# The last image of a window-attention block with a dynamic convolution: its mean and taps computed ahead, two convolution pieces as diagonal products

## The chip, the cores and the metric

The kernel runs on one core of a Trainium2 chip. The time is the device time of one execution in microseconds, the median over several runs. A core has five engines, each with a queue of its own: TensorE (PE, with its weight loads as PEld), VectorE (DVE), ScalarE (ACT), GpSimd (POOL) and SyncE (SP), which here only issues DMAs. ScalarE can issue DMAs too.

## The reference

```python
# layer 0: on x (16, 192, 56, 56), a shifted-window block (7x7 windows, 6 heads)
x1 = shortcut + window_attention(layernorm(x))
y  = gelu(layernorm(x1) @ fc1_w + fc1_b)           # 768 hidden channels
x  = x1 + (y @ fc2_w + fc2_b)
# layer 1: a depthwise 3x3 convolution whose taps depend on the image
pooled = x.mean(axis=(2, 3))                       # per image and channel
t  = relu(batchnorm(pooled @ w1.T))                # 48 values
wt = t @ w2.T + b2                                 # 9 taps per channel,
wt = wt * MASK                                     # of which 4 survive
out = depthwise_conv(x, wt, padding=1) + bias
```

The mask keeps the three taps of the row above and the left neighbour. So every output element is a bias and four products, and no output of an image can be computed before the mean over its whole final x is known. All data are fp32.

## The kernel before

The 16 images are cut into 4 units each (`NU`), 64 units in all. The 192 channels are 3 groups (`G`) of 64; the 128 partitions hold 64 channels of two halves of the image, 28 rows each (`LR`). So `x`, the residual and later the convolution's input, is a tile of 128 x 3 groups x 29 rows x 56, where row 0 is the halo: the last row of the other half, copied by two DMAs (L885). A unit is 7 rows of both halves.

The main loop (L1364 on) is a software pipeline over units: in round r it computes scores of unit r, the weighted sum and projection of r-1, the first MLP layer of r-2 (L783, GELU on ScalarE L795 into `hid`) and the second MLP layer of r-3 (L821, for each group 6 steps of two products, then on VectorE the update of x, L808, which also leaves the sum over the unit in `sums`). When the last unit of an image is through, `taps` follows: VectorE adds the unit sums to `pooled` (L843), TensorE multiplies by `w1` (L850), VectorE makes the taps `wt` (L861 to L879), and SP copies the halos (L885). Then `conv` runs for six pieces (half hf of the rows, group g), 14 rows of each partition: ScalarE writes the first tap with the bias (L911), VectorE adds the other three (L935, `scalar_tensor_tensor`, both inputs and the output in SBUF), ScalarE sets one row that lies at the top edge back to the bias (L928, pieces with hf = 1), and SP stores the piece in two or three DMAs (L948). For the last image there is nothing left to overlap with; its pieces are written into `hid`, which is free after the second layer has read it.

No engine's order is written down directly. Each step is an entry of `Plan` with an engine, a duration (its author's estimate), and the keys it reads and writes; `Plan.order` simulates the engines with these durations. TensorE keeps the order in which entries were added; on every other engine the step that could start first goes first, then the one that is due first. So durations and keys of an entry decide the order of all engines, and each engine then runs its list strictly in that order.

Of the kernel before, what the change touches and what calls it, by code (L numbers as in the profile page):

```python
# [45 lines left out]
class Plan:  # L46
# [95 lines left out]
def tile_swin_then_dynamic_conv(  # L142
# [37 lines left out]
    def sb(name, *shape):  # L180
        return const.tile(list(shape), F32, tag=name, name=name)
# [40 lines left out]
    m2 = sb("m2", 128, HT)  # L222
    rs = sb("rs", 128, HT)
    sums = [sb(f"sums{i}", 128, G, NU) for i in range(2)]
    pooled = sb("pooled", 128, G)
    trow = sb("trow", 128, RED)
    prod = sq.rearrange("p g t -> p (g t)")[:, 0 : G * NTAP * RED]
# [29 lines left out]
    def P(j):  # L257
        return slice(64 * j, 64 * j + 64)

    def X(s):  # L260

        b, u = divmod(s, NU)
        return [("x", b % 3, u, i) for i in range(3)]
# [534 lines left out]

            add("ACT", 0.95, go, [pk, "b1f", "table"], [("hid", f)])

    def second_layer(s):
        b, u = divmod(s, NU)
        xv = rows(s).rearrange("p g r c -> p g (r c)")
        for g in range(G):
            p, pk = bank()

            def ends(p=p, g=g):
                nc.vector.scalar_tensor_tensor(  # L808
                    xv[:, g],
                    p[:, 0, 0:UT],  # L810
                    vecs[:, 5, g : g + 1],
                    xv[:, g],
                    ALU.add,
                    ALU.add,
                    accum_out=sums[b % 2][:, g, u : u + 1],
                )

            for f in range(NFC):
                def product(p=p, g=g, f=f):
                    for ab in range(2):  # L820
                        nc.tensor.matmul(  # L821
                            p[P(ab), 0, 0:UT],
                            wf2[:, f, g * 64 : (g + 1) * 64],
                            hid[:, f, ab],
                            start=(f == 0),
                            stop=(f == NFC - 1),
                            tile_position=(0, 64 * ab),
                        )

                add("PE", 0.66, product, [("hid", f), ("wf2", f // 2)], [pk])  # L830
                if f == NFC - 1:
                    add("DVE", 0.65, ends, [pk, "vecs"], X(s) + [("sums", b % 2)])


    def taps(b):


        p, pk = bank()
        sl = b % 3
        add(  # L840
            "DVE",
            0.2,
            lambda: nc.vector.tensor_reduce(pooled, sums[b % 2], AX.X, ALU.add),  # L843
            [("sums", b % 2)],
            ["pooled"],
        )

        def product():
# [24 lines left out]
        w = wt[b % 2].rearrange("p g t -> p (g t)")  # L873

        def fin():
            nc.vector.tensor_reduce(
                w.rearrange("p (k o) -> p k o", o=1), prod, AX.X, ALU.add
            )
            nc.vector.tensor_tensor(w, w, b2t.rearrange("p g t -> p (g t)"), ALU.add)  # L879

        add("DVE", 0.9, fin, ["sq", "b2t"], [("wt", b % 2)])
        t = xt[sl]
        for to, of, row in ((0, 1, LR), (1, 0, LR)):
            def go(to=to, of=of, row=row):
                nc.sync.dma_start(t[P(to), :, 0, :], t[P(of), :, row, :])  # L885
            add("SP", 0.65, go, X(b * NU + NU - 1), [("halo", sl, to)], lag=2.5)

    pieces = [(hf, g) for hf in range(2) for g in range(G)]

    def conv(b, i):  # L890
        hf, g = pieces[i]
        sl = b % 3
        yi = (b * 6 + i) % 2
        y, yk = yt[yi], ("y", yi)
        if b == B - 1:

            y = hid[:, i].rearrange("p a (r c) -> p (a r) c", c=IMG)
            yk = ("hid", i)
        nr = LR // 2
        src = xt[sl][:, g]  # L900
        prev = src[:, nr * hf : nr * hf + nr]
        same = src[:, nr * hf + 1 : nr * hf + nr + 1]
        w = wt[b % 2]
        keys = [k for u in range(NU) for k in X(b * NU + u) if u // 2 == hf or u == 2 * hf - 1]
        if hf == 0:
            keys += [("halo", sl, 0), ("halo", sl, 1)]
        keys.append(("wt", b % 2))
        add(
            "ACT",
            1.05,  # L910
            lambda: nc.scalar.activation(  # L911
                y, prev, AF.Identity, bias=vecs[:, 6, g : g + 1], scale=w[:, g, 1:2]
            ),
            keys + ["vecs"],
            [yk],
        )
        for t, dst, s_ in (
            (0, y[:, :, 1:], prev[:, :, : IMG - 1]),
            (2, y[:, :, : IMG - 1], prev[:, :, 1:]),
            (3, y[:, :, 1:], same[:, :, : IMG - 1]),  # L920
        ):
            if t == 3 and hf == 1:

                r = IMG - SHIFT - LR - nr
                add(
                    "ACT",
                    0.35,
                    lambda: nc.scalar.activation(  # L928
                        y[64:128, r], zero[64:128], AF.Identity, bias=vecs[64:128, 6, g : g + 1]
                    ),  # L930
                    ["vecs", "zero"],
                    [yk],
                )
            def go(t=t, dst=dst, s_=s_):
                nc.vector.scalar_tensor_tensor(  # L935
                    dst, s_, w[:, g, t : t + 1], dst, ALU.mult, ALU.add
                )
            add("DVE", 1.4, go, keys, [yk])
        ch = slice(g * 64, g * 64 + 64)
        parts = [(0, 0, nr, SHIFT + nr * hf)]  # L940
        first = SHIFT + LR + nr * hf
        n = min(nr, IMG - first)
        parts.append((1, 0, n, first))
        if n < nr:
            parts.append((1, n, nr, 0))
        for h, lo, hi, at in parts:
            def go(h=h, lo=lo, hi=hi, at=at):
                nc.sync.dma_start(out[b, ch, at : at + hi - lo, :], y[P(h), lo:hi])  # L948
            add("SP", 0.65, go, [yk], [], lag=12.0)

    def table(name):
        add("ACT", 1.3, lambda: nc.scalar.preload_act_table_set(name), [], ["table"])
# [408 lines left out]
    def has(s):  # L1361
        return 0 <= s < S

    for r in range(-2, S + 3):  # L1364
# [57 lines left out]
        if norms:  # L1422
            deviations(norms)
        b, k = divmod(r - 3, NU)
        if k == NU - 1 and 0 <= b < B:
            taps(b)
        for b in range(B):
# [87 lines left out]
```

## Time and profile before

| | us |
|---|---|
| median of 3 runs | 2835.39 (2834.74 to 2842.21) |
| the profiled execution | 2838.8 |
| its span, first to last instruction | 2837.0 |
| PE busy | 2771.9 (98%) |
| DVE busy | 1857.8 (65%) |
| POOL busy | 1605.6 (57%) |
| ACT busy | 1562.2 (55%) |
| mean granted TensorE clock | 0.99 |

The span counts from the first to the last instruction that the profiler saw. The page says for each group of instructions how long one takes on the mean, how long its engine stood idle in front of it, and what ended that idle time; its chain of work that ended last says which engine the end hung on. The stretches view gives busy times between two moments of the span, with the clock that was granted to TensorE there (1.0 is full speed) and the DMA share. Waiting of an engine that nothing hangs on costs nothing.

### The profile page before, as it was taken

The page shows a single profiled execution, that of the slowest core. Times are in us where ns is not written, and L with a number is a line of the kernel's source. Part 1 is how long each engine was busy: PE and PEld are TensorE (multiplying, and loading weights), DVE is VectorE, ACT ScalarE, POOL GpSimd, SP SyncE. Part 2 cuts the span into 40 slices and gives each one's busy share as a digit, 9 for nine tenths or more (in the row PEclk, how much of TensorE's full clock was granted, in tenths as well). Part 3 has the DMA queues.
Part 4 walks back from the last instruction along what each step waited for, and adds up shares of the span by engine and source line. Part 5 has one row for each costly group of instructions (what it writes and reads, how often), then busy time and mean ns, then how long its engine had stood idle before and what let it go on. Part 6 is the DMA issues. An engine that isn't in the chain of part 4 may idle for free.

```text
span 2837.0 us, 79158 instructions
## 1 busy us (share of the span) xinstructions
PE 2771.9 (98%) x34241; PEld 1718.4 (61%) x34241; DVE 1857.8 (65%) x3129; ACT 1562.2 (55%) x2338; POOL 1605.6 (57%) x1424
## 2 busy tenths in 40 slices
PE   7899999999999999999999999999999999999995
PEld 5566666666566666566566566566566566566552
DVE  5565675767677586675767666576675767667564
ACT  3545556556556456556556556456555556556452
POOL 5564565565565565565665565565665665665530
PEclk9899999999999999999999999999999999999997
DMA  6312232323313324233333313324133332313121
GB/s 128 81 28 48 54 76 60 78 63 73 84 37 79 74 56 90 47 73 70 73 67 73 82 37 81 72 58 90 41 74 74 73 69 67 81 40 76 43 52 50
DMA packets 122229, 189.32 MB, mean 67 GB/s; under 512 B 31208, under 2 KB 96664, under 8 KB 121880
## 3 DMA queue, kind: packets, MB, share of 16 engines
q1 hardware_dynamic: 117512, 184.24, 29.2%
q8 instruction: 269, 4.41, 0.7%
q10 hardware_dynamic: 4368, 0.02, 0.1%
q14 instruction: 80, 0.66, 0.1%
HBM read 66.81 MB, written 38.98 MB: 37 GB/s over the span
## 4 chain that ended last, share of the span: by engine, by line
PE 96%; DVE 1%; DMA 1%; issue 1%; POOL 0%; ACT 0%; SPq 0%; ACTq 0%; DVEq 0%; POOLq 0%
PE ps L783 27%; PE ps L821 27%; PE ps L469 14%; PE ps L654 9%; PE ps L746 5%; PE ps L690 5%; PE ps L549 4%; PE ps L732 3%; PE ps L318 2%; DVE hid L935 0%; PE ps L850 0%; POOL xs L425 0%; SPq L1236 0%; ACT q L506 0%; PE ps L1115 0%
## 5 line engine op out<-in xcount | busy, mean ns | idle before, releaser
L821 PE MATMUL ps<-hid,wf 128*64 128x392 f32 x4608 | 772.5, 494 | 0.8 <-ACT o L717 0.8
L783 PE MATMUL ps<-xs,wf 64*128 64x392 f32 x4608 | 771.2, 490 | 2.1 <-POOL xs L454 2.1
L783 PEld LDWEIGHTS ps<-xs,wf 64*128 64x128 f32 x4608 | 446.5, 187 | 315.9 <-POOL xs L454 3.6
L821 PEld LDWEIGHTS ps<-hid,wf 128*64 128x64 f32 x4608 | 327.2, 137 | 411.2 <-issue 386.2
L302 POOL TENSOR_TENSOR fold<-sq 128x392 f32<-128x392 f32 x128 | 131.5, 1027 | 577.9 <-PE ps L318 509.7
L795 ACT ACTIVATE hid<-ps,b1f 128x784 f32<-128x784 f32 x384 | 341.5, 913 | 170.7 <-PE ps L783 168.6
L590 POOL TENSOR_TENSOR e<-e,top 128x784 f32<-128x784 f32 x192 | 306.2, 1610 | 216.4 <-DVE top L585 216.4
L469 PE MATMUL ps<-xs,wqkv 64*128 64x392 f32 x2304 | 404.0, 502 | 10.6 <-POOL xs L436 9.7
L935 DVE SCALAR_TENSOR_TENSOR y<-x,wt,y 128x770 f32<-128x770 f32 x270 | 329.5, 1234 | 86.1 <-ACT y L911 49.6
L482 ACT ACTIVATE q<-ps,qbs 128x400 f32<-128x400 f32 (+1 forms) x128 | 68.4, 589 | 493.6 <-PE ps L469 493.6
L608 POOL TENSOR_TENSOR e<-e,tot 128x784 f32<-128x784 f32 x192 | 307.3, 1614 | 49.3 <-DVE tot L603 47.1
L469 PEld LDWEIGHTS ps<-xs,wqkv 64*128 64x128 f32 x2304 | 221.6, 190 | 173.5 <-issue 18.6
L654 PE MATMUL ps<-wqkv,xs 64*64 64x192 f32 x6144 | 276.4, 325 | 0.0
L302 POOL TENSOR_TENSOR fold<-x 128x392 f32<-128x392 f32 x128 | 131.5, 1027 | 254.1 <-PE ps L318 166.7
L454 POOL TENSOR_TENSOR xs<-x,rb 128x392 f32<-128x392 f32 x192 | 236.9, 1261 | 30.1 <-DMA rb<-rsd 30.1
L717 ACT COPY o<-ps 32x392 f32<-32x392 f32 x512 | 246.5, 481 | 9.0 <-PE ps L690 2.7
L619 DVE STREAM_TRANSPOSE tt<-e 128x512 f32<-128x512 f32 x384 | 246.3, 685 | 5.1 <-POOL e L608 3.6
L654 PEld LDWEIGHTS ps<-wqkv,xs 64*64 64x64 f32 x6144 | 224.6, 133 | 29.0 <-issue 15.4
L575 DVE TENSOR_TENSOR e<-ps,bt 128x784 f32<-128x784 f32 x192 | 175.1, 968 | 99.2 <-PE ps L549 99.0
L770 DVE SCALAR_TENSOR_TENSOR x<-ps,pbt,x 128x196 f32<-128x196 f32 (+2 forms) x576 | 156.1, 344 | 96.5 <-PE ps L732 93.0
L602 DVE TENSOR_REDUCE tot<-e 128x16 f32<-128x784 f32 x192 | 180.4, 939 | 34.4 <-ACT e L597 34.3
L425 POOL TENSOR_TENSOR xs<-x,rb 128x343 f32<-128x343 f32 x192 | 186.5, 999 | 24.4 <-PE ps L654 17.4
(105 smaller groups left out, 3236.9 us busy)
## 6 DMA issues: line engine op xcount, KB each, us to landing
pt<-tt SPq DMA_DIRECT2D x256, 192.0 KB
x<-in_x_dram SPq DMA_DIRECT2D x112, 294.0 KB
out_dram<-y SPq DMA_DIRECT2D x135, 196.0 KB
pt<-tt SPq DMA_DIRECT2D x256, 96.0 KB
rb<-rsd SPq DMA_DIRECT2D x118, 196.0 KB
out_dram<-y SPq DMA_DIRECT2D x45, 154.0 KB
x<-in_x_dram SPq DMA_DIRECT2D x16, 168.0 KB
pt<-tt SPq DMA_DIRECT2D x128, 12.0 KB
```

The costliest lines, as they stand in the source:

```text
L302: nc.gpsimd.tensor_tensor(f, src[:, 0], src[:, 1], ALU.add)
L454: nc.gpsimd.tensor_tensor(xs2[:, g], xv[:, g], rb[:, 1], ALU.mult)
L469: nc.tensor.matmul(p[:, ab, 0:UT], lhs_qk(ab, g, i), d[P(ab), g, 0:UT], start=(g == 0), stop=(g == G - 1), tile_position=(64 * ab, 0),)
L590: nc.gpsimd.tensor_tensor(ev, ev, top[j].broadcast_to([128, 16, N]), ALU.subtract)
L608: nc.gpsimd.tensor_tensor(ev, ev, tot[j].broadcast_to([128, 16, N]), ALU.mult)
L619: nc.vector.transpose(tt[:, kb, 16 * j : 16 * j + 16], src)
L654: nc.tensor.matmul(p[P(w % 2), ab, i * DIM : (i + 1) * DIM], d[P(ab), g, w * N : w * N + 64], wqkv[P(ab), g, 2 * DIM :], start=(g == 0), s ...
L717: add("ACT", 0.5, lambda dst=dst, src=src: nc.scalar.copy(dst, src), [k], [("o", j, i)])
L783: nc.tensor.matmul(p[:, ab, 0:UT], wf1[P(ab), g, f * 128 : (f + 1) * 128], xs2[P(ab), g], start=(g == 0), stop=(g == G - 1), tile_position ...
L795: nc.scalar.activation(hid[:, f], p[:, :, 0:UT], AF.Gelu, bias=b1f[:, f : f + 1])
L821: nc.tensor.matmul(p[P(ab), 0, 0:UT], wf2[:, f, g * 64 : (g + 1) * 64], hid[:, f, ab], start=(f == 0), stop=(f == NFC - 1), tile_position= ...
L935: nc.vector.scalar_tensor_tensor(dst, s_, w[:, g, t : t + 1], dst, ALU.mult, ALU.add)
```

## The change

Only the last image is concerned; the instructions of all others keep their order.

1. *Early mean.* The mean of the last image no longer waits for the second layer's results. With the second layer linear, the sum over the last unit of `x + hid @ wf2 + fc2_b` is the sum of x (`xsum`, reduced before the update), plus the sum of each hidden channel (`hsum`, six reductions) times `wf2`, plus the bias times the number of positions. TensorE does 18 products of one column for it, between groups 0 and 1 of the second layer; the product with `w1` goes between groups 1 and 2.
2. *Dependences by group.* A piece of the convolution waits for its own group of x (`("fin", g)`) instead of for all of it.
3. *Two pieces on TensorE.* Pieces (1,1) and (0,2) are computed as four matmuls per 7 rows, with a diagonal 128 x 128 matrix of the tap as weights, shifted x as the moving side, accumulated in PSUM; ScalarE moves them to `hid` with the bias. GpSimd makes the eight diagonals from an identity and the taps. For (1,1) the row at the top edge is set to the bias by ScalarE and one row of VectorE puts its left-neighbour tap back.
4. *Stores on two queues.* These two pieces are stored by DMAs that ScalarE issues, the other four by SP.
5. *Durations* of the last image's VectorE steps go from 1.4 to 0.95 in the plan, the lag of its stores from 12 to 4, and the pieces are added in the order (1,1), (0,2), (1,0), (1,2), (0,0), (0,1).

As built, VectorE's list at the end reads: group 0's update, the product added to `pooled`, group 1's update, the taps, first step of (1,0), group 2's update, second step of (1,0), first and second of (1,2), third of (1,0), third of (1,2), first and second of (0,0), the row of (1,1), third of (0,0), the three of (0,1). ScalarE's reads: first tap of (1,0), of (1,2), their edge rows, first tap of (0,0), eviction and edge row of (1,1), first tap of (0,1), three stores of (1,1), eviction of (0,2), its two stores.

```diff
+    def early_mean(b):
+        s = b * NU + NU - 1
+        xv = rows(s).rearrange("p g r c -> p g (r c)")
+        for f in range(NFC):
+            add("DVE", 0.85, lambda f=f: nc.vector.tensor_reduce(
+                hsum[:, f : f + 1], hid[:, f].rearrange("p a t -> p (a t)"), AX.X, ALU.add),
+                [("hid", f)], [("hsum", f)])
+        add("DVE", 1.3, lambda: nc.vector.tensor_reduce(xsum, xv, AX.X, ALU.add), X(s), ["xsum"])
+        def go():
+            nc.vector.tensor_reduce(pooled, sums[b % 2][:, :, 0 : NU - 1], AX.X, ALU.add)
+            nc.vector.tensor_tensor(pooled, pooled, xsum, ALU.add)
+            nc.vector.scalar_tensor_tensor(
+                pooled, vecs[:, 5], float(UT), pooled, ALU.mult, ALU.add)
+        add("DVE", 0.5, go, [("sums", b % 2), "xsum", "vecs"], ["pooled"])
+        yield
+        p, pk = bank()
+        def product():
+            for g in range(G):
+                for f in range(NFC):
+                    nc.tensor.matmul(p[0:64, 0, g : g + 1], wf2[:, f, g * 64 : (g + 1) * 64],
+                        hsum[:, f : f + 1], start=(f == 0), stop=(f == NFC - 1),
+                        tile_position=(0, 0))
+        add("PE", 1.3, product, [("hsum", f) for f in range(NFC)], [pk])
+        add("DVE", 0.2, lambda: nc.vector.tensor_tensor(
+            pooled[0:64], pooled[0:64], p[0:64, 0, 0:G], ALU.add), [pk], ["pooled"])
...
+    def conv_product(b, i, unit, uk, room, dk):
+        hf, g = pieces[i]
...
+        for t in range(NTAP):
+            add("POOL", 0.35, lambda t=t: nc.gpsimd.tensor_scalar(
+                diag[:, t], unit, w[:, g, t : t + 1], None, ALU.mult),
+                uk + [("wt", b % 2)], dk if t == 0 else [("diag", g, t)])
+        p, pk = bank()
+        def product():
+            for j in range(2):
+                o = p[:, j, 0:UT].rearrange("p (r c) -> p r c", c=IMG)
+                r0 = nr * hf + j * WS
+                prev, same = src[:, r0 : r0 + WS], src[:, r0 + 1 : r0 + 1 + WS]
+                for k, (t, dst, s_) in enumerate((
+                        (1, o, prev),
+                        (0, o[:, :, 1:], prev[:, :, : IMG - 1]),
+                        (2, o[:, :, : IMG - 1], prev[:, :, 1:]),
+                        (3, o[:, :, 1:], same[:, :, : IMG - 1]))):
+                    nc.tensor.matmul(dst, diag[:, t], s_, start=(k == 0), stop=(k == NTAP - 1),
+                        skip_group_check=True)
...
+        add("PE", 5.3, product, keys, [pk])
+        add("ACT", 0.95, lambda: nc.scalar.activation(
+            y.rearrange("p (a r) c -> p a (r c)", a=2), p[:, :, 0:UT], AF.Identity,
+            bias=vecs[:, 6, g : g + 1]), [pk, "vecs"], [yk])
...
+        stores(b, hf, g, y, yk, "ACT", 3.0)
...
-            add("DVE", 1.4, go, keys, [yk])
+            add("DVE", 0.95 if b == B - 1 else 1.4, go, keys, [yk])
...
-        if has(r - 3):
+        if r == S + 2:
+            ahead = early_mean(B - 1)
+            next(ahead)
+            second_layer(S - 1, (0,))
+            for _ in ahead:
+                pass
+            second_layer(S - 1, (1,))
+            taps(B - 1)
+            second_layer(S - 1, (2,))
+            halos(B - 1)
+        elif has(r - 3):
             second_layer(r - 3)
...
-                for i in range(6):
+                unit = q2.rearrange("p w b c -> p (w b c)")[:, 0:128]
+                uk = [("q2", ab, h) for ab in range(2) for h in range(2)]
+                add("POOL", 1.0, lambda: make_identity(nc, unit), [], uk)
+                room = q128.rearrange("p a w b c -> p (a w b c)")
+                conv_product(b, 4, unit, uk, room, [("q128", h) for h in range(2)])
+                room = kbd.rearrange("p a w h t -> p (a w h t)")[:, 0 : NTAP * 128]
+                conv_product(b, 2, unit, uk, room, [("kbd", h) for h in range(2)])
+                for i in (3, 5, 0, 1):
                     conv(b, i)
```

More of the change, by code (lines that the diff above doesn't have):

```diff
@@ L224, in tile_swin_then_dynamic_conv @@
     sums = [sb(f"sums{i}", 128, G, NU) for i in range(2)]
+    hsum = sb("hsum", 128, NFC)
+    xsum = sb("xsum", 128, G)
     pooled = sb("pooled", 128, G)
@@ L799, in first_layer, with second_layer @@
             add("ACT", 0.95, go, [pk, "b1f", "table"], [("hid", f)])
-    def second_layer(s):
+    def second_layer(s, groups=range(G)):
         b, u = divmod(s, NU)
         xv = rows(s).rearrange("p g r c -> p g (r c)")
-        for g in range(G):
+        for g in groups:
             p, pk = bank()
@@ L831, in second_layer, with mean @@
                 if f == NFC - 1:
[L832 to L839, printed above, removed]
+                    add("DVE", 0.65, ends, [pk, "vecs"], X(s) + [("sums", b % 2), ("fin", g)])
+    def mean(b):
         add(
@@ L846, in taps @@
         )
+    def early_mean(b):
+        s = b * NU + NU - 1
+        xv = rows(s).rearrange("p g r c -> p g (r c)")
+        for f in range(NFC):
+            add(
+                "DVE",
+                0.85,
+                lambda f=f: nc.vector.tensor_reduce(
+                    hsum[:, f : f + 1], hid[:, f].rearrange("p a t -> p (a t)"), AX.X, ALU.add
+                ),
+                [("hid", f)],
+                [("hsum", f)],
+            )
+        add("DVE", 1.3, lambda: nc.vector.tensor_reduce(xsum, xv, AX.X, ALU.add), X(s), ["xsum"])
[3 more added lines that the diff above has]
+            nc.vector.scalar_tensor_tensor(
+                pooled, vecs[:, 5], float(UT), pooled, ALU.mult, ALU.add
+            )
+        add("DVE", 0.5, go, [("sums", b % 2), "xsum", "vecs"], ["pooled"])
[4 more added lines that the diff above has]
+                for f in range(NFC):
+                    nc.tensor.matmul(
+                        p[0:64, 0, g : g + 1],
+                        wf2[:, f, g * 64 : (g + 1) * 64],
+                        hsum[:, f : f + 1],
+                        start=(f == 0),
+                        stop=(f == NFC - 1),
+                        tile_position=(0, 0),
+                    )
+        add("PE", 1.3, product, [("hsum", f) for f in range(NFC)], [pk])
+        add(
+            "DVE",
+            0.2,
+            lambda: nc.vector.tensor_tensor(pooled[0:64], pooled[0:64], p[0:64, 0, 0:G], ALU.add),
+            [pk],
+            ["pooled"],
+        )
+    def taps(b):
+        p, pk = bank()
         def product():
@@ L881, in taps, with halos @@
         add("DVE", 0.9, fin, ["sq", "b2t"], [("wt", b % 2)])
+    def halos(b):
+        sl = b % 3
         t = xt[sl]
@@ L886, in taps, with first_row, stores, go @@
             add("SP", 0.65, go, X(b * NU + NU - 1), [("halo", sl, to)], lag=2.5)
+    def first_row(b, g, y, yk):
+        r = IMG - SHIFT - LR - LR // 2
+        add(
+            "ACT",
+            0.35,
+            lambda: nc.scalar.activation(
+                y[64:128, r], zero[64:128], AF.Identity, bias=vecs[64:128, 6, g : g + 1]
+            ),
+            ["vecs", "zero"],
+            [yk],
+        )
+    def stores(b, hf, g, y, yk, eng, lag):
+        nr = LR // 2
+        parts = [(0, 0, nr, SHIFT + nr * hf)]
+        first = SHIFT + LR + nr * hf
+        n = min(nr, IMG - first)
+        parts.append((1, 0, n, first))
+        if n < nr:
+            parts.append((1, n, nr, 0))
+        ch = slice(g * 64, g * 64 + 64)
+        q = nc.sync if eng == "SP" else nc.scalar
+        for h, lo, hi, at in parts:
+            def go(h=h, lo=lo, hi=hi, at=at):
+                q.dma_start(out[b, ch, at : at + hi - lo, :], y[P(h), lo:hi])
+            add(eng, 0.65, go, [yk], [], lag=lag)
@@ new lines, in conv_product @@
+    def conv_product(b, i, unit, uk, room, dk):
+        hf, g = pieces[i]
+        nr = LR // 2
+        src = xt[b % 3][:, g]
+        w = wt[b % 2]
+        y = hid[:, i].rearrange("p a (r c) -> p (a r) c", c=IMG)
+        yk = ("hid", i)
+        diag = room.rearrange("p (t c) -> p t c", c=128)
+        for t in range(NTAP):
+            add(
+                "POOL",
+                0.35,
+                lambda t=t: nc.gpsimd.tensor_scalar(
+                    diag[:, t], unit, w[:, g, t : t + 1], None, ALU.mult
+                ),
+                uk + [("wt", b % 2)],
+                dk if t == 0 else [("diag", g, t)],
+            )
+        p, pk = bank()
+        def product():
[3 more added lines that the diff above has]
+                prev, same = src[:, r0 : r0 + WS], src[:, r0 + 1 : r0 + 1 + WS]
+                for k, (t, dst, s_) in enumerate(
+                    (
+                        (1, o, prev),
+                        (0, o[:, :, 1:], prev[:, :, : IMG - 1]),
+                        (2, o[:, :, : IMG - 1], prev[:, :, 1:]),
+                        (3, o[:, :, 1:], same[:, :, : IMG - 1]),
+                    )
+                ):
+                    nc.tensor.matmul(
+                        dst, diag[:, t], s_, start=(k == 0), stop=(k == NTAP - 1),
+                        skip_group_check=True,
+                    )
+        keys = [("fin", g)] + dk + [("diag", g, t) for t in range(1, NTAP)]
+        if hf == 0:
+            keys += [("halo", b % 3, 0), ("halo", b % 3, 1)]
+        add("PE", 5.3, product, keys, [pk])
+        add(
+            "ACT",
+            0.95,
+            lambda: nc.scalar.activation(
+                y.rearrange("p (a r) c -> p a (r c)", a=2),
+                p[:, :, 0:UT],
+                AF.Identity,
+                bias=vecs[:, 6, g : g + 1],
+            ),
+            [pk, "vecs"],
+            [yk],
+        )
+        if hf == 1:
+            first_row(b, g, y, yk)
+            r = IMG - SHIFT - LR - nr
+            add(
+                "DVE",
+                0.2,
+                lambda: nc.vector.scalar_tensor_tensor(
+                    y[64:128, r, 1:],
+                    src[64:128, nr + r + 1, : IMG - 1],
+                    w[64:128, g, 3:4],
+                    y[64:128, r, 1:],
+                    ALU.mult,
+                    ALU.add,
+                ),
+                [("fin", g), ("wt", b % 2)],
+                [yk],
+            )
+        stores(b, hf, g, y, yk, "ACT", 3.0)
@@ L906, in conv @@
             keys += [("halo", sl, 0), ("halo", sl, 1)]
+        if b == B - 1:
+            keys = [("fin", g)] + (keys[-2:] if hf == 0 else [])
         keys.append(("wt", b % 2))
@@ L922, in conv @@
             if t == 3 and hf == 1:
[L924 to L933, printed above, removed]
+                first_row(b, g, y, yk)
             def go(t=t, dst=dst, s_=s_):
@@ L937, in go @@
                 )
-            add("DVE", 1.4, go, keys, [yk])
[L939 to L949, printed above, removed]
+            add("DVE", 0.95 if b == B - 1 else 1.4, go, keys, [yk])
+        stores(b, hf, g, y, yk, "SP", 4.0 if b == B - 1 else 12.0)
     def table(name):
@@ L1424, in tile_swin_then_dynamic_conv @@
         b, k = divmod(r - 3, NU)
-        if k == NU - 1 and 0 <= b < B:
+        if k == NU - 1 and 0 <= b < B - 1:
+            mean(b)
             taps(b)
+            halos(b)
         for b in range(B):
```

## The prediction

> **What bounds the kernel now.** I read the page's chain that ended last first: 96% of it is TensorE, so the body of the run is bound by matmuls that the change doesn't touch. Then I read the same chain over the last 32 us, and the busy times by stretch, to see where TensorE stops being the bound.
>
> ```profile
> 2784.60:2795.00 10.40, 10.40 (x66) 5.80 (x64) 0.00 (x0) 4.57 (x5) 0.00 (x0) 1.00 0.01 2
> 2795.00:2807.10 12.10, 11.98 (x72) 4.99 (x72) 1.27 (x4) 2.20 (x2) 0.00 (x0) 1.00 0.00 0
> 2807.10:2811.30 4.20, 0.87 (x6) 0.74 (x6) 2.89 (x8) 0.00 (x0) 0.00 (x0) 1.00 0.11 22
> 2811.30:2824.70 13.40, 0.00 (x0) 0.00 (x0) 12.29 (x14) 6.71 (x9) 0.00 (x0) 0.52 0.00 0
> 2824.70:2837.00 12.30, 0.00 (x0) 0.00 (x0) 4.58 (x5) 0.00 (x0) 0.00 (x0) 0.50 0.69 196
> ```
>
> Columns: stretch, its length, busy us of PE, PEld, DVE, ACT, POOL, then PEclk, DMA share, GB/s. TensorE is full until 2807.1. Then come 30 us in a row: 4 us for mean and taps, 13 us in which VectorE alone works at the convolution and no byte is stored, 12 us of stores. GpSimd is idle throughout. The rows of the tail:
>
> ```profile
> L935 DVE SCALAR_TENSOR_TENSOR hid<-x,wt,hid 128x770 f32<-128x770 f32 x18 | 16.9, 1016 | 1.2 <-ACT hid L911 1.2
> L911 ACT ACTIVATE hid<-x,vecs,wt 128x784 f32<-128x784 f32 x6 | 5.7, 1028 | 14.1 <-DVE wt L879 14.1
> 2807.13 0.63 DVE L808 SCALAR_TENSOR_TENSOR x<-ps,vecs,x 128x392 f32<-128x392 f32 x1 [3.32 <-PE ps L821]
> 2824.68 9.66 SPq L948 DMA_DIRECT2D out_dram<-hid  x15
> ```
>
> Eighteen VectorE steps at a cadence of 16.9/18 = 0.94; they go tap by tap over all six pieces, so the first piece is whole at 2824.6. Then SP issues 15 stores, one per 0.64 us, until 2834.34. The landing events put 2.7 us (a lone store) to 3.1 us (in the stream) between the start of a 196 KB issue and its landing, and 1.1 us between the last landing (2835.9) and the end.
>
> **The change, on the time line of this execution.** Span 2837.0, run 2838.8; the median of the runs shown is 2835.4, 3.4 less. I compute the new end in the span and take the difference off the median.
>
> Covered, cost nothing: the reduction of x before its last update (1176 elements; from 0.94 for 784, 1.4 us) falls where VectorE was idle 9.5 us before 2766.2; the six reductions of hid (0.94 each) follow GELUs 1.97 apart in a stretch where VectorE had been idle 19.4 us. The last one ends at 2796.9, before the first group's products (2798.9). Uncovered they would cost 1.4 and 5.6. The identity (0.6 us at most by the memset and select rows) waits on GpSimd for the last read of q2, with the last unit's score steps queued behind it; these themselves wait for VectorE until 2706.8, 2 us after that read. The order of all older work, SP's too, is unchanged.
>
> *Mean and taps.* The second layer's three groups take 12.07/3 = 4.0 us of PE each, their updates of x start at 2799.2, 2803.2 and 2807.1. Between groups 0 and 1 come 18 products with one column: 36 passes of 64 weight columns. The nearest rows:
>
> ```profile
> 52.89 4.18 PE L1097 MATMUL ps<-vecs,wf 64*128 64x1 f32 x36
> 87.00 0.28 PE L1177 MATMUL ps<-bv,wp 128*64 128x1 f32 x2
> 115.13 1.58 PE L383 MATMUL ps<-fold,hid 128*128 128x392 f32 x4
> ```
>
> 36 passes of 128 columns take 4.2, 0.112 each; in the second line two passes of 64 columns start 0.055 apart. Ends 2.0 and 4.2; I take 2.0 plus 0.1 at the switch. Group 1's update then starts at 2803.2+2.1 = 2805.3. The tap product (0.67 to issue) is ready by 2805.9, while VectorE is in that update; it follows at 2805.95, and from there to the taps it is 2.24 as now (2808.99 to 2811.23): taps at 2808.2, 3.0 earlier. Group 2 ends late: its update can start at 2807.1+2.1+0.7 = 2809.9.
>
> *VectorE's half.* ScalarE's first step waits for the taps and for group 2's read of hid 3 (2808.6); VectorE follows 1.07 later, 2809.7. Then 12 steps instead of 18, the update of group 2 (0.63, queued second) and a row of 55 (0.25). But the cadence of 0.94 belongs to independent neighbours: where a step needs the one just in front, it starts 1.05 after (1.015 and a gap of 0.035, as in the taps' chain). The written order has four such pairs: +0.5. In front of the second piece's first step stands ScalarE's step, which waits for group 2's update (2811.4): VectorE goes on at 2812.5. From there: ten steps and the row, 10 x 0.94 + 0.4 + 0.25 = 10.1, the end at 2822.6. The halo copies (issued 2811.4, landed 2.7 later as now) are in at 2814.1; ScalarE turns to them at 2814.9, so they hide. The row waits on ScalarE's eviction of the first product piece, with four steps and the last stores queued behind it; needed at 2818.4, there at 2817.4: 1.0 of slack.
>
> *Diagonals on GpSimd.* No row shows this form. By the two-input rows (0.33 for 63 elements, 1.0 for 343) 128 elements cost 0.49; the Trainium skill (GPSIMD Engine Reference, "Engine selection" and the per-element model under it) has one-input work roughly at line rate, 1.03 cycles an element at 1.2 GHz, 0.11 plus the rows' fixed 0.17: 0.28. I take the row, nothing here shows the faster rate. Eight take 3.9 (2.2 by the rule), 2808.3 to 2812.2; the first two, all that the first matmul needs, are there at 2809.3, before PE is free at 2809.6. So they cost PE nothing by either. They cost VectorE something, since a step with two SBUF inputs is held up beside GpSimd:
>
> ```profile
> L935 DVE SCALAR_TENSOR_TENSOR y<-x,wt,y x270: 977/1021/2252, 321.1 to 2775.8; 128x770 f32<-128x770 f32 x135
> L935 DVE SCALAR_TENSOR_TENSOR hid<-x,wt,hid x18: 1012/1015/1021, 2812.4 to 2828.3; 128x770 f32<-128x770 f32 x18
> ```
>
> (Shortest, median, longest: 2252 beside GpSimd, 1015 in the tail where it is idle.) Two steps meet a diagonal, each waiting at most one, 0 to 1.0 in all: 0.2, since ScalarE's wait takes up most of it.
>
> *TensorE's half.* By the L383 line 4 passes take 1.58, 0.33 each and a tail of 0.17. A piece is 16: 5.3. Pieces end at 2815.0 and 2820.3 (halos and diagonals are in before each). The first one's three issues (0.6 each) stand on ScalarE ahead of the second's eviction, from 2818.3 to 2820.1: 0.2 of slack. Then eviction (1.0) and two issues: the last from 2822.0. VectorE is later.
>
> *Stores.* Ten remain on SP. The piece last done (2822.8 with the 0.2) is issued at 2822.8 and 2823.4; earlier ones are out by then, as pieces now become whole one by one from 2815.4. Last issue 2823.4 + 3.1 (four stores close together, as in the stream; 2.7 if they don't press) + 1.1 = 2827.6, or 2827.2. So 9.4 to 9.8 off: **2826.0** from the median, about 2829.4 for a profiled run like this one.
>
> **Rivals.**
>
> *The clock drops (0.22).* This bears on the row of one-column products:
>
> ```profile
> 2779.00:2781.20 2.20, 0.10 (x4) 0.02 (x2) 0.63 (x2) 0.00 (x0) 1.08 (x2) 1.00 0.79 229
> 2781.20:2784.60 3.40, 3.40 (x10) 1.79 (x12) 0.00 (x0) 0.00 (x0) 1.87 (x2) 0.50 0.00 0
> 53.00:57.30 4.30, 4.30 (x37) 4.20 (x38) 4.08 (x7) 3.16 (x8) 3.44 (x4) 1.00 0.40 82
> 57.40:60.70 3.30, 3.30 (x14) 2.44 (x13) 2.49 (x7) 1.04 (x4) 2.72 (x3) 0.50 0.00 0
> ```
>
> After 2.2 us without matmuls the clock ran at half for 3.4 us; after 4.3 us of one-column products, PE "busy" throughout, the same. So these products don't count as work. The Trainium skill (TensorE: Matmul & The Clock Gate, "Why this matters for your kernels") sees trouble only from idle gaps over some 3 us: by it, 2.1 us of such products cost 2.1. By the row they may cost half a window more, 1.7: 2827.7. With 4.2 us of them, 2829.9. It speaks for the rival that the gap equals the one that dropped; against it, that the drop at 2781 came only as 3.4 us held 1.3 of work, so the gap must fall whole into one such window.
>
> *PE becomes the bound (0.06).* If a pass had to wait for its weights (0.19), a piece would be 16 x 0.52 = 8.3: pieces end at 2817.9 and 2826.2, last issue 2827.9, end 2832.1: 2830.5. L383's line speaks against it.
>
> *Shorter (0.06).* No holding-up (0.2), the row of 55 and the switch hidden (0.35), and stores that land in 2.7 or in 2.1 (as the last, small one did): 2825.0 or 2824.4.
>
> *Slower than before (0.03).* A diagonal on GpSimd is far dearer than its rows. The second piece's first half needs the eighth; behind it stand 5 matmuls (3.3), eviction, an issue, 4.2. From 2808.3, the end passes 2837.0 once eight cost over 19.5, 2.4 each; at 4.0 the end is 2849.5, 2847.9 on the median. All rows of this size are under 0.5.
>
> *The change does nothing* (0.01): the pieces would have to end together again, but the written order of VectorE ends them one by one.
>
> **Numbers.** The forecast case has 0.62, 2825.3 to 2827.5. 0.3% (about what a measurement of this kernel can tell from no change) is 8.5 us: faster means under 2826.9. From the cases: 0.53 of the forecast's 0.62, the shorter case and a little of the clock's give 0.60; the rest of the forecast, the clock's, PE's and 0.01 for no effect, 0.37; slower 0.03. The range 2824.4 to 2829.9 takes in the forecast, the clock and the shorter case, and leaves out 0.1.
>
> **What would show it.** Right: taps 3 us earlier; one-column products some 2.1 us; a VectorE step train that ends near 2822.8; diagonals under 0.5; first store near 2815.4; PE's pieces 5.3 each. Wrong: PEclk 0.5 behind the one-column products, two-input steps well over 1.05 in the train, VectorE waiting at the row of 55, or stores that land over 3.1 after their issue because two queues press the DMA at once.

## The result, and the profile after

The change takes 2829.42 us (median of 7 runs, 2824.54 to 2832.60). The kernel before, run beside it, took 2838.19 (median of 7, 2834.74 to 2842.21). The ratio is 0.9967, 95% interval [0.9955, 0.9978]: 9.4 us faster, by the interval between 6.2 and 12.8 (the medians alone differ by 8.8). The forecast of 2826.0 was taken off the median of three runs (2835.39), which lay 2.8 lower than that of seven. So the measured median lies 0.5 under the upper end of the stated range (2829.9) and outside the forecast case (2825.3 to 2827.5), while the gain, 9.4 to 9.8, is what the ratio shows. The profiled execution took 2829.52, its span is 2827.7 (before 2838.8 and 2837.0): 9.3 less, where the working ended at 2827.2 to 2827.6. That the two spans can be compared so directly is luck: the last unit's second-layer products start at 2794.91 and 2794.92 in them, and anywhere from 2784.5 to 2797.0 in the kernels of the experiments.

Busy times by stretch of the changed kernel (stretch, length, busy PE, PEld, DVE, ACT, POOL, then PEclk, DMA share, GB/s):

```profile
2784.60:2795.00 10.40, 10.40 (x66) 5.89 (x64) 4.84 (x5) 4.58 (x5) 0.00 (x0) 1.00 0.01 2
...
2799.00:2801.20 2.20, 2.20 (x40) 2.16 (x39) 0.67 (x3) 0.00 (x0) 0.00 (x0) 1.00 0.00 0
2801.20:2810.00 8.80, 8.80 (x55) 4.69 (x51) 2.87 (x9) 1.04 (x1) 1.50 (x3) 1.00 0.00 1
2810.00:2815.40 5.40, 5.40 (x19) 3.24 (x18) 5.27 (x7) 1.96 (x4) 5.17 (x6) 1.00 0.08 16
2815.40:2820.60 5.20, 5.20 (x17) 2.71 (x15) 5.10 (x7) 2.98 (x4) 0.00 (x0) 1.00 0.68 187
2820.60:2827.70 7.10, 0.02 (x1) 0.00 (x0) 2.40 (x3) 0.91 (x1) 0.00 (x0) 0.83 0.66 205
```

The first row holds five of the six reductions of hid (DVE 4.84, before 0.00) and PE is as full as before: they are covered. The one-column products are the second row, and the clock stays at 1.00 through it. Where before had 13.4 us with only VectorE and ScalarE at work and no byte stored, PE, VectorE, ScalarE and GpSimd now work side by side for 5.4 us, and after that the stores (187 GB/s) run beside the convolution. From VectorE's last step to the end of the span it is now 4.6 us, where it was 7.7.

The timeline of the same kernel (start, length, engine, line):

```profile
2798.92 2.15 PE L878 MATMUL ps<-hsum,wf 128*64 128x1 f32 x35
...
2805.63 0.63 DVE L810 SCALAR_TENSOR_TENSOR x<-ps,vecs,x 128x392 f32<-128x392 f32 x1 [4.31 <-PE ps L823]
...
2808.24 0.17 DVE L931 TENSOR_TENSOR wt<-wt,b2t 128x12 f32<-128x12 f32 x1
...
2809.96 5.46 PE L1006 MATMUL ps<-x,q 128*128 128x392 f32 x16
...
2815.77 8.47 SPq L969 DMA_DIRECT2D out_dram<-hid  x10
```

The products take 2.15, group 1's update starts at 2805.63, the taps are ready at 2808.41 (before 2811.23), PE's first piece starts right behind group 2, and the first store is issued at 2815.77 (before 2824.68). The last of SP's ten issues starts at 2823.65 (before 2833.79) and lands 2.97 later; the span ends 1.1 after that.

The rows of the new work, from the trace by line (shortest, median, longest ns; first and last start):

```profile
L985 POOL TENSOR_SCALAR q<-q,wt x4: 605/606/1130, 2808.5 to 2810.2; 128x128 f32<-128x128 f32 x4
L985 POOL TENSOR_SCALAR kbd<-q,wt x4: 599/1068/1132, 2811.4 to 2814.1; 128x128 f32<-128x128 f32 x4
```

```profile
L1085 DVE SCALAR_TENSOR_TENSOR hid<-x,wt,hid x12: 1009/1020/1160, 2809.9 to 2822.0; 128x770 f32<-128x770 f32 x12
```

A diagonal costs 0.6 alone and 1.1 beside a two-input VectorE step, not 0.49. VectorE has 12 steps of 1.02 in the median where it had 18 of 1.015; two of them (1.16 and 1.13) were held up beside GpSimd.

### The profile page after: what moved, and what is told of

Its sections match the earlier page's. It is cut to its first block, busy times and chain, and to the rows that moved or that the text cites. A ratio compares the mean times of both kernels' runs of the same rounds, so it can differ in the third digit from the quotient of the medians.

```text
span 2827.7 us, 79305 instructions
## 1 busy us (share of the span) xinstructions
PE 2788.3 (99%) x34309; PEld 1729.1 (61%) x34309; DVE 1861.3 (66%) x3134; ACT 1563.2 (55%) x2338; POOL 1613.1 (57%) x1434
## 4 chain that ended last, share of the span: by engine, by line
PE 97%; DVE 1%; POOL 1%; DMA 1%; issue 0%; ACT 0%; SPq 0%; ACTq 0%; POOLq 0%; DVEq 0%
PE ps L785 27%; PE ps L823 27%; PE ps L471 14%; PE ps L656 9%; PE ps L748 5%; PE ps L692 5%; PE ps L551 5%; PE ps L734 3%; PE ps L320 2%; PE ps L902 0%; POOL xs L427 0%; DVE hid L1085 0%; PE ps L1237 0%; PE ps L1255 0%; PE ps L385 0%
## 5 line engine op out<-in xcount | busy, mean ns | idle before, releaser
L823 PE MATMUL ps<-hid,wf 128*64 128x392 f32 x4608 | 773.0, 494 | 0.3 <-issue 0.3
L823 PEld LDWEIGHTS ps<-hid,wf 128*64 128x64 f32 x4608 | 327.9, 137 | 409.2 <-issue 382.9
L456 POOL TENSOR_TENSOR xs<-x,rb 128x392 f32<-128x392 f32 x192 | 236.1, 1257 | 30.2 <-DMA rb<-rsd 30.2
L604 DVE TENSOR_REDUCE tot<-e 128x16 f32<-128x784 f32 x192 | 180.4, 940 | 34.6 <-ACT e L599 34.5
```

The costliest lines, as they stand in the source:

```text
L456: nc.gpsimd.tensor_tensor(xs2[:, g], xv[:, g], rb[:, 1], ALU.mult)
L823: nc.tensor.matmul(p[P(ab), 0, 0:UT], wf2[:, f, g * 64 : (g + 1) * 64], hid[:, f, ab], start=(f == 0), stop=(f == NFC - 1), tile_position= ...
```

## Experiments

The runs of one kernel spread over some 8 us, and in the profiles nearly all of that lies ahead of the last image's end: the start of the last unit's second-layer products, from 2784.5 to 2797.0, lies in kernels whose work ahead of them differs by nothing that fills these 12 us. So the kernels are compared by their **tail**, from the start of those products (L823, before L821) to the end of the span: 42.1 before, 32.8 after, a difference of 9.3. All times below "into the tail" count from there. Each kernel has one profile. That the tail itself repeats shows in VectorE's first convolution step, which starts 14.96 to 14.97 into the tail in five kernels with the early mean and 17.50 to 17.51 in five without, and in the run times: for all seven kernels with an interval below that have the body of before or of the change, the difference of the tails lies inside it. The theory at the outset was the prediction's sum: early taps, six VectorE steps fewer, pieces whole one by one, and an end that hangs on VectorE's last step. The rivals: the order of the steps does it alone; the second queue does it; the clock or GpSimd takes something back.

| kernel | tail | VectorE's last step ends | last issue of a store | ratio to before, 95% interval |
|---|---|---|---|---|
| before | 42.1 | 34.4 | 38.9 | 1 |
| the change | 32.8 | 28.2 | 28.7 | 0.9967 [0.9955, 0.9978] |
| e3_order_only | 42.9 | 34.5 | 38.8 | 0.9999 [0.9991, 1.0008] |
| e2_all_on_vector | 39.8 | 32.4 | 35.6 | 0.9992 [0.9985, 0.9998] |
| e1_no_early_mean | 38.8 | 30.5 | 34.8 | 0.9992 [0.9984, 0.9999] |
| e4_one_queue | 34.4 | 28.3 | 30.2 | 0.9970 [0.9957, 0.9982] |
| f3_order_only_in_order | 39.7 | 35.4 | 35.9 | 1.1602, other body, see there |
| f2_all_on_vector_in_order | 37.8 | 33.4 | 34.0 | 1.1595, other body |
| f1_no_early_mean_in_order | 36.9 | 30.6 | 31.6 | 1.1589, other body |
| e5_sum_twice | 38.6 | 33.7 | 34.3 | single run, no interval |
| e6_diagonals_on_vector | 34.6 | 28.2 | 30.8 | single run, no interval |
| e10_diagonals_twice | 38.0 | 31.7 | 33.9 | single run, no interval |
| e8_two_tiles_two_queues | 32.3 | 27.2 | 27.3 | 0.9961 [0.9947, 0.9975] |
| e7_two_tiles | 32.1 | 27.1 | 27.7 | 0.9968 [0.9956, 0.9980] |

**The parts undone.** e3: neither the early mean nor the products.

```diff
-        if r == S + 2:
-            ahead = early_mean(B - 1)
...
-        elif has(r - 3):
+        if has(r - 3):
             second_layer(r - 3)
-        if k == NU - 1 and 0 <= b < B - 1:
+        if k == NU - 1 and 0 <= b < B:
             mean(b)
-                conv_product(b, 4, unit, uk, room, [("q128", h) for h in range(2)])
...
-                conv_product(b, 2, unit, uk, room, [("kbd", h) for h in range(2)])
-                for i in (3, 5, 0, 1):
+                for i in (3, 4, 5, 0, 1, 2):
```

> Undoes the early mean and the products: mean and taps after all three groups, all six pieces on ScalarE and VectorE, stores on SP. What is left of the change is the written order (pieces become whole one by one). The measure is the tail, from the start of the last unit's second-layer products (L823) to the end of the span: 42.05 us before, 32.78 after. The sum: taps as before (2811.2), 18 steps from 2812.4 at 0.94 with some nine dependent neighbours at 0.11 more each, so the last step ends near 2830.3, last issue 2830.9, then the 4.05 of the tail of after: 40.0, 2 shorter than before. Rival, the gain is mostly the overlap of the stores that the order brings: 36 or less. Rival, the order brings nothing: 42.

It gave 42.9, near the 42 of the rival "the order brings nothing". The timeline of this kernel says why:

```profile
2808.86 16.97 DVE L1085 SCALAR_TENSOR_TENSOR hid<-x,wt,hid 128x770 f32<-128x770 f32 x18 [1.19 <-ACT hid L1071]
...
2821.21 9.50 SPq L969 DMA_DIRECT2D out_dram<-hid  x15
```

18 steps in 16.97 is the cadence of independent neighbours, and the first store goes out 12.35 after the first step: the steps still stand tap by tap over all pieces, and the stream of 15 stores (0.64 each) ends last. My expectation was wrong on its premise: this kernel is not in the order that I took it to have. (It is 0.8 longer than before since its last store, of 196 KB, landed 3.1 after its issue; before's last, of 42 KB, 2.1.)

e2: the early mean kept, the products undone (the last part of the diff above).

> Keeps the early mean and taps and the written order; undoes the two product pieces (all six pieces on ScalarE and VectorE, all stores on SP, no diagonals). The sum: train from 2809.9, six steps more than after at 0.94 to 1.05, no row of 55 (0.3) and no hold-up by GpSimd (0.25): last step ends near 2828.3, last issue 2829.0, tail 38.2 (after 32.8). So the products would be worth some 5.4, the early mean 1.8 on top of the order alone. Rival, the stores and not VectorE set the end: then six steps more fall behind the stores and the tail is below 36. Rival, the early mean is worth its full 2.8: tail 37.2.

39.8, longer than any of the three. VectorE ends at 32.4, early enough for 37.1 (0.65 to the last issue, then 4.05), but after the first piece (whole at 22.1) the next store is issued only at 28.7, and 12 stores then follow one another to 35.6. Again the order.

e1: the early mean undone (the first part of the diff), the products kept.

> Undoes the early mean alone: mean and taps come after all three groups as before; the two product pieces, the diagonals and the second queue stay. The sum: taps at 2811.2 in place of 2808.4, but the update of group 2 no longer lies in the train of convolution steps, and ScalarE need not wait for it: VectorE's end 1.8 later than after, tail 34.6. Rival, the whole shift of the taps counts: 35.6. Rival, the early mean gives back what its one-column products cost (2.1): tail within 0.5 of after, 32.8 to 33.3.

38.8, 6.0 longer than the change and longer than any theory had it.

```profile
2809.18 8.27 DVE L1085 SCALAR_TENSOR_TENSOR hid<-x,wt,hid 128x770 f32<-128x770 f32 x8 [1.19 <-ACT hid L1071]
...
2818.32 3.81 DVE L1085 SCALAR_TENSOR_TENSOR hid<-x,wt,hid 128x770 f32<-128x770 f32 x4
...
2819.40 7.80 SPq L969 DMA_DIRECT2D out_dram<-hid  x10
```

VectorE ends 2.3 later in the tail than in the change (I had said 1.8), but the first whole piece comes after nine steps, and ten stores leave in a heap. The order on the engines comes from the planner (L73 to L120), which takes of the steps that are ready the one due first. In the change the taps come ahead of the halo rows (13.5 and 19.3 into the tail), so that only the two pieces without halos are ready, and these are finished first. With late taps the halos are already there (15.6, the taps at 16.3), all four pieces are ready together, and the planner goes tap by tap. So the early mean does two things, of which the prediction counted one.

**The order held.** To part them, VectorE's steps were given due times piece by piece:

```diff
-    def conv(b, i):
+    def conv(b, i, due=None):
...
-            add("DVE", 0.95 if b == B - 1 else 1.4, go, keys, [yk])
+            by = None if due is None else due
+            due = None if due is None else due + 1.0
+            add("DVE", 0.95 if b == B - 1 else 1.4, go, keys, [yk], by=by)
...
-                    conv(b, i)
+                    conv(b, i, 1.0 + 3.0 * n)
```

A due time is handed back to all that an operation waits for (L84 to L90), so that the planner wrote the whole run in another order and the body became some 450 us longer. These three kernels say something by their tails alone; VectorE's first step stands in them where it stands in their counterparts (17.5, 15.0 and 17.5 into the tail).

> As the run with neither the early mean nor the products (tail 42.9), but with VectorE's 18 steps put piece by piece by due times. Theory: VectorE starts at 17.5 into the tail, 18 steps at 0.94 and some ten dependent neighbours at 0.11 make 18.0, last issue 0.65 later, then 4.05: tail 40.2, 1.9 shorter than before (42.05). Rival, the 15 stores on one queue are the bound in any order: 42 or more. Rival, what the change gains is mostly this order: 36 or less.

> Early mean and taps, no product pieces, all six pieces on ScalarE and VectorE, now piece by piece by due times (tail 39.8 in the planner's own order). Theory: train from 15.0 into the tail, the update of group 2 in it (0.6), 18 steps and neighbours 18.0, then 0.65 and 4.05: 38.2. Against the run with the order alone (expected 40.2) the early mean is then worth 2, and the products 5.4 against after (32.8). Rival, the stream of stores is the bound: 39.8 again.

> As the run without the early mean (tail 38.8, where 34.6 was expected), but VectorE's convolution steps are put in the order piece by piece by due times, which the late taps had turned into an order tap by tap. Theory: the tail is the later of VectorE's end + 0.6 + 4.05 and the stream of stores that starts with the first whole piece; with the order mended VectorE starts at 17.5 into the tail and needs 12.7 (12 steps, some neighbours, the row of 55, 0.6 of hold-up): tail 34.9, or 35.3 by the second product piece, whose diagonals come late. Then late taps alone cost 2 to 2.5 and the order the other 3.5. Rival, the late taps themselves cost all 6: 38.8 again. Rival, the stores' slots (a semaphore of ScalarE's store that SP has to wait for, 1.25 us in that run) are the cause: 37.6.

f3 gave 39.7 (40.2 expected), f2 37.8 (38.2): right, VectorE is the bound there. The timeline of f3:

```profile
3270.00 17.84 DVE L1085 SCALAR_TENSOR_TENSOR hid<-x,wt,hid 128x770 f32<-128x770 f32 x18 [1.19 <-ACT hid L1071]
...
3273.97 15.02 SPq L969 DMA_DIRECT2D out_dram<-hid  x15
```

The same 18 steps now take 17.84 (dependent neighbours), 0.87 more than in e3, but the first store leaves 4.0 after the first step instead of 12.35, and the tail is 3.2 shorter. f1 gave 36.9: VectorE's end (30.6) and the last issue (31.6) are near what the theory had (30.2, and 30.8 or, by the second product piece, 31.2), but the last landing came 4.2 after the last issue. Four stores of 196 KB, two on each queue, were issued between 30.7 and 31.6; their packets moved from 31.8 to 35.4, 784 KB in 3.6 us. So the path was right and the landing mis-sized. The trace also shows why the four stores met:

```profile
3267.18 7.25 PE L1006 MATMUL ps<-x,q 128*128 128x392 f32 x16 [3.68 <-POOL q L985]
```

With late taps PE has 5.6 us between the second layer and its first piece (the tap product of 0.87 and the 3.68 in front of the diagonals lie in them). The clock is at 0.50 from 14.5 to 21.3 into the tail, and the first piece takes 7.25 instead of 5.46 (in e1 7.34). By an estimate from these two figures the second piece's two stores were issued 1.8 later than at full clock, among SP's last two instead of ahead of them. So the early mean does a third thing: it leaves PE no such gap. How much of the tail this is worth was not tested by itself. SP's wait of 1.25 for a semaphore last used by a store of ScalarE's, seen in e1, is gone in f1; but as the order changed with it, its own share stays open.

So, with the order held, the 9.3 us part into: order alone 2.4 (42.1 to 39.7), early mean and taps 1.9 (to 37.8), the two product pieces with their own queue 5.0 (to 32.8). The early mean is worth more beside the products: 4.1 by f1, where the half clock is a part of it, and 6.0 by e1, where the planner changes the order as well.

**The second queue.** e4 issues the product pieces' stores on SP.

```diff
-        stores(b, hf, g, y, yk, "ACT", 3.0)
+        stores(b, hf, g, y, yk, "SP", 4.0)
```

> The five stores of the product pieces go to SP's queue like the others. The sum: 15 issues of about 0.63 in a row from 2815.8 put the last issue at 2824.6 to 2824.9 in place of 2823.65: tail 33.8 to 34.0, 1.0 to 1.25 longer than after. Rival, the second queue is worth nothing since SP waits for VectorE before its last two stores anyway: 32.8. Rival, two queues press the DMA and one queue lands sooner (2.7 after the issue in place of 2.97): 33.5.

34.4, 1.6 longer. VectorE ends as in the change (28.3), but SP's row of 15 runs to the end, without the wait for VectorE that stands in the change ahead of the last two:

```profile
2816.55 10.14 SPq L969 DMA_DIRECT2D out_dram<-hid  x15
```

The last issue is 1.5 later, a little more than 1.25, since the two issues ahead of it took 0.69 and 0.78. The sum holds, and the tail fits neither rival (32.8, 33.5). In run times the two kernels can't be told apart (0.9970 and 0.9967).

**The one-column products.** e5 does them twice over; e7 and e8 spread them over two column tiles.

```diff
+                for _ in range(2):
                     for f in range(NFC):
```

> The one-column products are done twice over (72 passes in place of 36; the second pass writes the same sums again). Theory by time alone: 2.1 us more, tail 34.9. Rival, the clock: 4.2 us in which these products count as no work hold a whole window, PE then runs at half clock for 3.4 us inside group 1 or 2 and the tail is 36.6.

38.6: dearer than both. Stretches of this kernel, in the columns used above:

```profile
2784.50:2788.50 4.00, 4.00 (x26) 1.77 (x25) 1.07 (x2) 2.20 (x2) 0.00 (x0) 1.00 0.00 0
2788.50:2792.80 4.30, 4.30 (x70) 4.25 (x68) 0.63 (x2) 0.00 (x0) 0.00 (x0) 0.91 0.00 0
2792.80:2796.20 3.40, 3.40 (x16) 2.40 (x17) 0.15 (x1) 0.00 (x0) 0.00 (x0) 0.50 0.00 0
2796.20:2799.50 3.30, 3.30 (x14) 2.12 (x12) 0.00 (x0) 0.00 (x0) 0.00 (x0) 0.59 0.02 5
```

In the second row the one-column products run, with PE "busy" to the last; 3.5 us after their start the clock falls to half (at 2792.05), and it stays there for 6.83 us, not for the 3.4 that I had priced. The taps are 5.4 later than in the change: 2.1 of time and 3.3 of clock. The clock rival is real, and twice as dear as forecast; at 2.1 us of such products none of five profiles showed it (the change, e2, e4, e6, e10).

```diff
                 for f in range(NFC):
+                    ab = f % 2
                     nc.tensor.matmul(
-                        p[0:64, 0, g : g + 1],
+                        p[P(ab), 0, g : g + 1],
...
-                        start=(f == 0),
-                        stop=(f == NFC - 1),
-                        tile_position=(0, 0),
+                        start=(f < 2),
+                        stop=(f >= NFC - 2),
+                        tile_position=(0, 64 * ab),
...
-            lambda: nc.vector.tensor_tensor(pooled[0:64], pooled[0:64], p[0:64, 0, 0:G], ALU.add),
+            lambda: nc.vector.tensor_tensor(pooled, pooled, p[:, 0, 0:G], ALU.add),
```

e8 adds to this that in the last piece's stores the queue becomes ScalarE's after the first one.

> The change, with two additions: the one-column products lie alternately in two column tiles of PE (partitions 0 to 63 and 64 to 127 of the sum), and the last piece's second store goes to ScalarE's queue. Theory: tiles in different columns run side by side, so 2.1 us of products become 1.05 and everything after moves up by that; the last issue no longer stands 0.5 behind the one before it: tail 31.2 (after 32.8). Rival, the products are bound by the rate at which PE takes instructions and not by their tile: 32.2. Rival, the last store's landing is bound by the DMA stream and not by its issue: 31.7.

> The change with the one-column products in two column tiles of PE, but with the last piece's two stores on SP as in the change. In the run before this one, which also split those two stores over two queues, the products took 1.05 less as expected, VectorE ended 0.93 earlier and the last issue came 1.45 earlier, but the tail was only 0.5 shorter than after (32.3 against 32.8). Theory: the split cost 0.45, since the two stores then move side by side and each takes longer; without it the tail is 31.8. Rival, the split is neutral and the stream of stores is full anyway: 32.3.

```profile
2794.84 1.17 PE L879 MATMUL ps<-hsum,wf 128*64 128x1 f32 x36
```

In e8 all 36 passes take 1.17: the tiles do run side by side. The taps are 1.05 earlier in both kernels, VectorE ends 0.9 to 1.0 earlier. Of that 0.5 arrives in e8 and 0.7 in e7; from the last issue to the last packet it takes 2.9 in e7 and 3.4 in e8, against 2.6 in the change. The likely reason, not tested by itself, is that the earlier stores now stand closer to the last and the stream of stores is nearly full. Splitting the last two stores gained nothing (it may have cost 0.2, which two profiles can't settle). So e8 comes out at the number of its first rival (32.2), though the rival's reason, no gain from two tiles, is refuted by the 1.17. Both are the shortest tails found; in time they can't be told from the change (intervals in the table).

**The diagonals.** e6 makes them on VectorE, e10 makes each twice over on GpSimd.

```diff
             add(
-                "POOL",
-                0.35,
-                lambda t=t: nc.gpsimd.tensor_scalar(
+                "DVE",
+                0.25,
+                lambda t=t: nc.vector.tensor_scalar(
```

> The eight diagonals are made on VectorE, ahead of its convolution steps, in place of GpSimd. Theory: eight at some 0.2 fall into the 1.5 us in which VectorE waits for ScalarE's first step, and VectorE's two-input steps are no longer held up (0.25): tail 32.5 to 32.9. Rival, GpSimd takes real work off VectorE: 34.4.

The trace of e6 by line:

```profile
L985 DVE TENSOR_SCALAR q<-q,wt x4: 281/282/286, 2808.2 to 2808.8; 128x128 f32<-128x128 f32 x4
L985 DVE TENSOR_SCALAR kbd<-q,wt x4: 281/281/282, 2809.0 to 2810.5; 128x128 f32<-128x128 f32 x4
```

VectorE makes a diagonal in 0.28, one every 0.2, and its last convolution step ends at 28.2 in the tail, as in the change: making them on GpSimd takes no time off VectorE here. The tail is 1.8 longer all the same, and the rival's number (34.4) is met for a reason that isn't the rival's. The planner again wrote another order: a piece of the lower half that is whole by 22.8 into the tail in the change becomes whole at 27.2, so that five of SP's stores leave after 27.2, and one of their issues took 1.5 us. What diagonals on VectorE would give in the order of the change was not run.

```diff
+            for _ in range(2):
                 add(
                     "POOL",
                     0.35,
```

> GpSimd makes each diagonal twice over (16 steps in place of 8, the same values). It tests the slack that the prediction gave to the diagonals: the eighth would be there at 15 us after the taps in place of 6.7, PE's second piece would end near 29.9+4 into the tail, then eviction, two issues and the landing: tail 37.5, and VectorE's two-input steps are held up for longer (1.1 in place of 0.94, some 0.6 more). Rival, GpSimd's work is covered in full: 32.8. Rival, the hold-up of VectorE is what matters: 33.5.

38.0 (37.5 expected): the cover is gone. The timeline of e10:

```profile
2812.73 7.92 PE L1007 MATMUL ps<-x,q 128*128 128x392 f32 x16 [4.13 <-POOL q L986]
...
2814.76 6.52 POOL L986 TENSOR_SCALAR kbd<-q,wt 128x128 f32<-128x128 f32 x8
...
2820.49 5.36 PE L1007 MATMUL ps<-x,kbd 128*128 128x392 f32 x16
...
2822.00 0.28 DVE L1034 SCALAR_TENSOR_TENSOR hid<-x,wt,hid 64x55 f32<-64x55 f32 x1 [3.51 <-ACT hid L950]
```

PE waits 4.13 for the diagonals and then needs 7.92 instead of 5.46, part of it at half clock (0.50 from 2810.9, still in that gap, to 2817.7); VectorE stands 3.51 at the row of 55, the wait that the prediction had named with 1.0 of slack. Eight diagonals at 0.83 in the mean are covered; sixteen are not. The 38.0 thus holds both the wait and the slower clock behind it, which the expectation did not have.

## Why the prediction was right, step by step

- **Covered reductions**: right. The stretch from 2784.6 to 2795.0 has PE full.
- **One-column products, 2.0 + 0.1**: right (2.15). Group 1's update was forecast for 2805.3 and began at 2805.63; the 0.3 between them isn't explained.
- **Taps at 2808.2**: 2808.41. **VectorE's start at 2809.7**: 2809.89, with the update of group 2 queued behind its first step as said. **The second piece's first step at 2812.5**: 2812.62.
- **Dependent neighbours at 1.05, hold-up 0.2**: right; 1.05 is seen in four pairs, and the two held-up steps cost 0.14 and 0.11. VectorE's end, 2822.8 with the hold-up: 2823.07.
- **Diagonals at 0.49, eight in 3.9**: this term of the sum was mis-sized. They take 0.58 from start to start alone and 1.06 to 1.13 beside VectorE's two-input steps, 6.66 for eight (2808.51 to 2815.17). The two-input rows that I scaled from were no near row for it. The 0.28 that I estimated from the Trainium skill's per-element model (GPSIMD Engine Reference, "Elementwise — side-by-side cycle accounting") lay further off still. The error cost nothing because the first two were there before PE, and the eighth is first needed some way into PE's second piece, which began at 2815.26. The prediction's "slower" rival had worked out that slack; e10 shows that twice the work is not covered.
- **PE's pieces, 5.3 each**: 5.46 and 5.36, ends 2815.4 and 2820.6 (said 2815.0 and 2820.3). The 5.3 left out the tail of 0.17 that its own line has; with it the sum is 5.45.
- **Stores**: last issue 2823.65 (said 2823.4), landing 2.97 (3.1), end 1.1 (1.1). e4 shows what the second queue is worth, 1.6 of the tail.
- **The clock rival**: it didn't come in the profiled run. Its reason, that these products don't count as work, fits e5, where the clock fell while PE was shown as busy with these products alone; what it is in them that the clock doesn't count stays open. Its price was too low for 4.2 us of them (3.3 measured, 1.7 said).
- **What the prediction left out**: it read the order of the steps from the built kernel, rightly, but took that order as given. By e1, e2, e3 and e6 the order hangs on when the planner finds the taps and the halos ready. It also did not see that early taps spare PE a gap and so the half clock (f1, e1). For the sum this made no difference; for the question which part brings the gain, it does.

## What to carry to other kernels

Where the end of a kernel is compute and then a stream of stores, write the compute so that outputs become whole one after another: here the same 18 steps in that order were 0.87 slower in themselves and shortened the tail by 3.2. Where a planner writes the order, a change in when one input is ready can rewrite it, so look at the order of every variant before its time is credited to the part that was changed. And compare such kernels from a fixed mark near the end, if the body's own spread is as large as the effect.

## What the runs showed of the hardware

- In 4.2 us of one-column products (e5), with PE shown as busy, the clock fell to 0.5 after 3.5 us and stayed there for 6.83 us; with 2.15 us (five profiles) and 1.17 us (e7, e8) of them it did not fall. Behind 5.6 us in which PE had 0.87 of work (f1, e1), and behind 4.13 us in which it had none (e10), the first product piece ran in part at 0.5 and took 7.25 to 7.92 us instead of 5.46.
- A 128x128 f32 multiplication by a value per partition takes GpSimd 0.605 us, and 1.06 to 1.42 beside VectorE's steps with two inputs; VectorE 0.281, one every 0.2.
- One-column products in two column tiles run side by side: 36 passes in 1.17 us instead of 2.15.
- Issues of 0.6 us on SP stretched to 1.2 and 1.5 in e6 and to 0.8 in e4, while other stores were under way; four stores of 196 KB issued within 1.0 us on two queues (f1) landed up to 4.4 us after their issue, the last two of the change, on one queue, 3.0.
